# A mixture-of-experts kernel on one core: experts ranked for each set of tokens, weights reloaded in that order, raw token rows

## The chip, the core and the metric

The kernel runs on one core of a Trainium2 chip. Its engines are TensorE (PE, matrix products and transposes), VectorE (DVE), ScalarE (ACT), GpSimd (POOL, which also issues the indirect transfers) and SyncE (SP, which issues nearly all other transfers); sixteen DMA engines carry out what the queues are given. The metric is the time of one execution on the device in microseconds (us), as the median of several runs.

## The reference, cut to what matters

4096 tokens (16 sequences of 256) of width 128 pass four residual steps:

```
x = x + attention(layernorm(x))      # softmax weights summed over m and multiplied by v of the same token
x = x + ffn(layernorm(x))            # layer 1
x = x + mixer(layernorm(x))          # selective scan with 16 states, and the skip term u * D
x = x + ffn(layernorm(x))            # layer 2

ffn: logits = x @ gate_w             # 8 experts
     top 2 of 8, softmax over the two
     h = relu(x @ w1[e])             # 128 -> 512
     y = h @ w2[e]                   # 512 -> 128
     out = sum over the two of weight * y
mixer: y = scan(u, delta, A, B, C) + u * D;  out = y @ W_out + b_out
```

In the attention the softmax weights of a token sum to one over m, so that it reduces to the projection of v. Both layers use the same gate and expert weights. All values are float32.

## The kernel before

**Tiling.** Tokens are worked on in 8 blocks of TB = 512, four tiles of 128 rows each, which stay in SBUF (`xs_[b]`). A layer goes through its blocks in sets: `FIRST = ([0], [1], [2, 3], [4, 5], [6, 7])` in layer 1 and `SECOND = ([0, 1], [2, 3], [4, 5], [6], [7])` in layer 2. For each set, `route` picks two experts per token, works out with a running count (a matmul with a triangle) which slot of which expert each token gets, and scatters the token rows by indirect DMA into a DRAM buffer `slots`. `experts` then goes through the eight experts: it fetches the expert's slots (tile `xs`), transposes them (`xsT`), multiplies with w1 (`up`, PSUM `ps_b` or `ps_B`, then relu into `h`) and w2 (`ps_y`, `yT`), transposes back (`yr`) and stores them in a DRAM buffer `ys`. `collect` gathers for each token its two result rows (`yy`) and adds them to x. The first set of layer 1 has no slots in DRAM: `dealt` builds one-hot matrices and gathers by a matmul. Between the layers stands the mixer; at the end `finish` transposes and writes the output.

**Rooms.** Each expert position r of a set has a fixed room of K x C rows, given in `SLOTS` as (K, C): K is the number of partitions of the tiles `xs` and `yr`, and C the number of rows on each. The PE computes on all K x C columns, used or not. Rooms have to be as large as the number of tokens that any expert in this position gets. `beyond` collects by how much a set overflows, and if any does, a general path computes everything anew after the end. Where K is over 116 or C is 1 (`byrow`), the second product gives rows and needs no second transpose.

**Ranking.** `RANKED = (2,)`: at the first set of layer 2 the experts are ranked by the number of tokens in that set. From then on position r means the expert of rank r; `load_experts` reads its number into a register of SP and loads its weights once for all sets of the layer. In layer 1 the experts have their natural order and equal rooms. `w1_s` and `w2_s` have one buffer for each of the eight positions, 256 KB each.

**Slots in DRAM.** A row's address interleaves the experts: row i of expert e is at i * 8 + e, so a partition's C rows lie apart and each row moves as 512 B.

```
            return t[0 : NE * n * c].rearrange("(p c e) w -> e p c w", e=NE, c=c)[r]
```

**Scaling.** The token rows are normalized and multiplied with their routing weight before they are scattered (tile `row`: one ACT or DVE operation of 128 x 128 for each tile and choice), which relu lets pass. The results are added as they are.

**The order.** The functions do not issue instructions. They record jobs in a `Plan`, each with the tiles it reads and writes, the engines that may do it (`either`), and for transfers an assumed duration (`took`). The string `ORDER` holds a rank for each job and, where there is a choice, the engine; the plan then emits every job in order, with the semaphore waits that follow from it. So all instructions of the profile stand on the one line L772, except the indirect transfers (scatter L880, gather L892), the loads of ranked weights (L934, L940), and filler matmuls (L1705) which are put where the plan expects the PE to be idle. SP is one in-order queue: the loads of weights, the fetches of `xs`, the stores of `ys` and the output stand in it one behind the other, and one that waits holds up the others. POOL is likewise one queue for scatters, gathers and its own arithmetic. `xs` and `yr` have four buffers each (`XS`).

Of the kernel before, what the change touches and what calls it, by code (L numbers as in the profile page):

```python
# [11 lines left out]
BF16 = mybir.dt.bfloat16  # L12
# [7 lines left out]
P = 128  # L20
# [15 lines left out]
        2: ((108, 3),) * 8,  # L36
    },
    {
        "first": ((126, 3), (112, 3), (108, 3), (98, 3), (96, 3), (88, 3), (126, 2), (117, 2)),
        1: ((98, 2), (91, 2), (88, 2), (80, 2), (84, 2), (75, 2), (70, 2), (128, 1)),  # L40
        2: ((126, 3), (117, 3), (110, 3), (104, 3), (108, 3), (96, 3), (90, 3), (126, 2)),
    },
)
RANKED = (2,)
UNIT = 2
JOIN = 2

COLD = 5.0
# [14 lines left out]
    "c-qZZ2V4_p|G(!F2uWCBZ^GVNMD}nMWhmmpRjsY4t)oufI_lQiswi$nt>RvFf>K)%!~%*UB1=HoJFEa1cmE`Jxw{}(`+wi}^LZ0U"  # L63
    "a?kVJZ+?H@-|v>G_^I*=>c6NNCEAl^pxer^W>rkfI9&R;>iv%8rd7`B9lu02joA1NUDGqgsne+5m*>sC|3s_)i)v%K>WE364%f`z"
    "G%9VWd>|BeK0IC08FfuyS$#TV!ssUsJvZ9pw@tBaV2TlOKM(^Ype&9CWvPXsXYyKG+Pu%zXlZI1Sm&A}IY4CALbDer*&iR4gwV&l"
    "%_}jzc_s5zX!X3PvIWf#4x)X!&c}M*s#~aW*_FM4<>R>>-Ss7LRsE&oXUE3!i@n2)%YK;$2Ux%Q=KJd&AzO97EXmqll<=(G$|n86"
    "dYcDRExkEyN=&Uj^@^>Aca=O|2u`0WZ*KkZPp*nx>bjin<VsZC<o=9uRhFUFl+z=MPhNm~zw4pXzFM^_s$-IHUykn8ElEaxc^26-"
    "@4I$-U9_@v4^`W~w0Z1KeP?YmwJLUVr{|Jk*2t*vvi=>escnr%S2%5T@YvyUd1cK_&1T~j6D^|8^}R6ZVc4@5r`2UVu#9lkK^d>j"
    "<5raWMYj1fEzYZOy26KDMUnzv7Ki#3$Js3MGeWdkH_RQX!$+g^SGwX*L0g)m*&ht^hr`B{m+-Z+MtiQ=%kQlyO?ID9`_|x>g>x4a"
    "7{0aWT9KvwE7Mny<Gx<_BC^rwXq|G-%~+*L?XOC-N_X*TlWs>d*t>6dr4MgmZ>V5Cdl#UwvuaJIa7A;6SkO9NyAy2)R#I*_c4irG"  # L70
    "f$}i1aA)c7s#VilXwygk=1!Yh4K5@zA4WBp!hdS2*QXZDe|&PBD<YV-*P?Y!iDl#0qE3S>ix*QK?M<<E=x(XAp(VMh1?XG@R;LUe"
    "^+r5mvX*|O{~BSeh+)#r_1}t5_Zhr&a6Vyi`WybF4oh}yO!N4+5htCOsU-6w+usb|b1Ki@BBPCK;{T?1ty+gYBRIVexWd-=;yaSJ"
    "&s)c$pQk1Mu(kK>{gXydj2^f9i*!A>vkJ$Aory7?vCXs9d*QbqY<=vPD_5viZHRw+xyi_Maei$clW%G}<<Bhkhz`r&MH-;Cg^e&a"
    "U3gYoEtvixd0S^(bWqX_ezZ?DQW4gCxKZW)U-sXiwFV<^9XWugj&I$OH!^<jINSI_Rp(0X8CAy1J2}<+XY8MsQOzx+FI`ck!)UF1"
    "r{3=xWR>+`>d7lshLx35&odZn7Zx}mrDnxJanplDErz>)?7F~R3+C+aA5-pJSJA{omZhmanOZhgkCAfdi0_(u)pB)q^G@34(G14f"
    "eS4#Xe51_BB9U#NK~YP9t>|iZM^tyo*>WS%F&D1MxJN(sPW#RtZCBBJZJ^)!epUT0n_AeiD}P#^{fyO-2NJ+a(?751T|Dt?cbC&s"
    "Vc(n$QTC>HM#at;b;t51I;SD3MmT%!f%h}4>PBvxuFe>3;@b3@A8^VmYfe%~m6J|SeG|jhc2S6Tkp)nnb$DNx$-9k@&62&})9eDh"
    "ScjD#Mm+6S`}*KmrOj)ty&MV-D)rOH_rKCv)^PRbMmOGYj!yTV8??Q`+N`UlY#O%f5B};74O>|C*7x@ozso+too$4EyDPAtJ-2Le"
    "uTEEI%<mI*o7jdlVWH_fj=;E{yK8^RlKf4p9e+HX@qI@>qK&dre+c0=@TMCTa6xyst-wJ;H>2N&$y}<c%!q`U@CUzomIp^G>DPJt"
    "S!x=E$jI-zmAMAtYp?dBF3J<a_^i}!9^FgHm{tEc#Gh9&w{A|0ef5VbPi>8y1=e34J|A%@QR|nJJQv~V+30jzx^DxA@33*RbCs>%"  # L80
    "ef3A`HOopwyjkjeHH}(F$Ieng4b!X;HExa5f1%a}jGt%hF>5F+ZFknJV%x@_61{ioY8P?EddV{*+HUb(fS#Qbt)^2r^(WJ`)UPYu"
    ")JFWl;98WeIb=8Tk2<=R1-&Pa79=`8w;g#um40nvvTte-sCm{D_|vkM$>|}6bRG!cYgMZ0^S*OreBm=TH+%Z~Jcp5~?Y_@P(9st@"
    "2CsX<E{?mh@~%t6aDJ(4L*w;>xy$qNjg9mfd=Ae^*L+-(bAJ8d=)3ycVdKZQ%egm9ODFqhX5N_LFyCI_K3f0nvJ^FDW!RAzPKVo+"
    "&IIVELnF5YsV!Rmvh`YcsoiL^-lwHm!S_vG?p9glT3%@%v(D~K^6D*%ik-FG(>9-*)PGiwXO`l5rF63Hy$X+bo)u_IOW1QRTiI}<"
    "<_VqfqH_^joC>Np-yO~piB@y!^DI<vt(p<a79|+4%EN6Q+BDz2GK+27_hV+{U*BnPFSKTUHNV=Vhjk($xUov;CwT7HHq%es;o@7v"
    "s~x8lM&||AjNuQ<wZ6Bmwd>bY8~1<UXj(W%Ur`$cXWJOv-;lnhYT8?FUx$uYp|x^`un9G&o1Iu;t!dRW&g^Bb=_0hyX(rG0_x5<J"
    "W}lxb*X~)HAE-1pB;BQ^LG!O|{!7wateXuPjy1g47G;AAOE#v|-`IO4l;JX=Le)SmG4aUQQQ6kXA%1z9t<NK0dmq^jAGBJpuKxgd"
    "eXkawFZ5$JMr2mlKB{8c=h)_Zy$KD=PPGs%xvk#g-~MD_9aH;}d%czM@ozmdc5X7%n7k(1V&fu#xkh5jB_tPq;C45@tIXzkaGgr;"
    "`U-V}elJ1K5|2t9!%F4Ie79N)zMgFdqAF5lr;az799pBdl=r?p=s{9t<;`CXoASO{t7VrlBRG@0J_1I0K8Wt`_lI$swmu6BI^+PG"
    "R<t`R#ilQeDPFoWaTfD_W-45&V`fle={DiT+;e$tuyA_JGv2os@98-1FqqaFKEJbL>3+MFs}kA@zjoxM2@bBZ-Zv|~*-qnO412%B"  # L90
    "Hrl?39I;U2Nl)*kc{(>WG8$)ax|gm~8_)17zHBvazRBVuOO~Pjb<fxgT5}Y$rBU13yY<|T>gT@6y{t2fvzNc1KieD~H?c3yIG5%1"
    "EZC;L<sGZu9pMPV16%ccCfxd9<XECrYvkB!<h1ocr=`%<`N@intL=VX)*h7_ooi=p!&4c>U}btmTfv<omWIQ-a$8N>Cfiq*;mz*K"
    "X~Rn9R^2?n+niWz_x`eL{ozpO&1-+YWLh^$VDQqHpSVriI0n@^F|pk#E1}=9&or)NWV*op*e;vXrU5-JJxh-3Fk{-vL_ZWd-(`H2"
    "k@>2&TjXi*rq>P$e>>}7fV!t%UxR&U@8s&d;UV$g>F5|2Zpc2S=4zO^Jm5y+3zK*Htk~qyL5(?+wC+!_Zq6Cy`MkJ=^V`TyeWuXt"
    "&YapiOGBTs*#<0g<ztSzO#Mb4*Oi?TS!SZ4o^E#ZOhD4zQ=R+|Ixbw%HSS}*_Wf~Z>nrHuK4p{B+fH~UE>nKqtaR_P_PR4V=)GIP"
    "!Ikr-C#gjoJ>T&4m`N)*+szxBUi?zstQE)^-*auA<Lrx}7Gn-|ZG9f9D$<H~iw)(J4uc)c&AfL9uaDPpx~_b%G&X4U1Ad5jy|0kt"
# [1679 lines left out]
```

## Time and profile before

| | |
|---|---|
| median of 3 runs | 469.81 us (469.47 to 470.01) |
| the profiled execution | 467.84 us, span 466.1 us, granted clock 0.994 |
| busy, share of span | PE 96%, DVE 74%, ACT 58%, POOL 67% |
| DMA | 55.37 MB, mean 119 GB/s |
| fetches of `xs`, stores of `ys` | 72 and 80 |
| loads of weights | 32 of 256 KB |
| indirect transfers | 120 scatters, 128 gathers |

The profile is one execution, seen by the hardware's profiler. The span runs from the first to the last instruction; the time of the execution has 1.7 us around it. An engine's busy time is the sum of its instructions. Matmuls are pipelined and the ends of their records are modelled, so the mean duration of a matmul is larger than the distance from one start to the next. A float32 matmul leaves two records (two passes over the columns).

### The profile page before, as it was taken

How to read it: one execution, taken by the hardware profiler on the slowest of the kernel's cores; microseconds unless marked ns; L12 is line 12 of the kernel's file. 1: busy time of each engine (PE TensorE's matmuls, PEld its weight loads, DVE VectorE, ACT ScalarE, POOL GpSimd, SP SyncE). 2: the span in 40 equal slices, each digit the busy share in tenths (PEclk: the TensorE clock that was granted, in tenths of full speed). 3: DMA queues.
4: the chain of work that ended last, by engine and by line, in shares of the span. 5: the costliest groups of instructions: out<-in, count | busy, mean ns of one | idle time of the engine just before them, and what ended most of it. 6: DMA issues, size and time to landing. Idle time of an engine off the chain costs nothing.

```text
span 466.1 us, 8797 instructions
## 1 busy us (share of the span) xinstructions
PE 447.0 (96%) x2670; PEld 355.8 (76%) x2670; DVE 345.6 (74%) x1229; ACT 268.3 (58%) x621; POOL 311.8 (67%) x482
## 2 busy tenths in 40 slices
PE   8999999999999999989997999989999999999994
PEld 6889998866766667665665777677678877999993
DVE  4799999778697878999999998996786931223420
ACT  2124443577576854995889496797735534343310
POOL 8188787777673761276866776836785477778662
PEclk9999999999999999999999899999999999999999
DMA  5974234632352423236644322144225333543251
GB/s 155 340 244 135 71 122 134 166 107 66 108 155 67 114 78 96 65 106 195 188 121 142 93 73 76 53 120 132 69 58 146 114 113 90 135 125 91 78 164 45
DMA packets 74917, 55.37 MB, mean 119 GB/s; under 512 B 8184, under 2 KB 66800, under 8 KB 74864
## 3 DMA queue, kind: packets, MB, share of 16 engines
q1 hardware_dynamic: 66640, 38.35, 28.5%
q0 software_dynamic: 7936, 16.27, 12.1%
q8 instruction: 23, 0.38, 0.4%
q14 instruction: 30, 0.25, 0.2%
q10 hardware_dynamic: 288, 0.13, 0.1%
HBM read 28.95 MB, written 25.77 MB: 117 GB/s over the span
## 4 chain that ended last, share of the span: by engine, by line
PE 72%; DVE 16%; ACT 4%; issue 3%; POOL 2%; DMA 1%; POOLq 0%; DVEq 0%; ACTq 0%
PE ps_b L772 25%; PE ps_y L772 24%; PE ps_B L772 21%; DVE x L772 3%; DVE ps_B L772 2%; DVE stats L772 2%; PE ps_y L1705 2%; POOL yy L892 2%; DVE w L772 1%; DMA yy<-ys,of 1%; DVE th L772 1%; ACT th L772 1%; DVE rt L772 1%; ACT decay L772 1%; DVE u L772 1%
## 5 line engine op out<-in xcount | busy, mean ns | idle before, releaser
L892 POOL DMA_INDIRECT yy<-ys,of x128 | 125.5, 980 | 64.4 <-issue 37.2
L880 POOL DMA_INDIRECT slots<-row,to x120 | 120.6, 1005 | 49.5 <-issue 19.4
L772 PE MATMUL ps_y<-h,w_s 128*128 128x324 f32 (+13 forms) x552 | 145.2, 382 | 0.0
L772 PE MATMUL ps_B<-xsT,w_s 128*128 128x324 f32 (+9 forms) x352 | 112.8, 442 | 0.8 <-DVE w L772 0.4
L772 PEld LDWEIGHTS ps_y<-h,w_s 128*128 128x128 f32 x552 | 90.4, 190 | 20.3 <-issue 1.3
L772 PEld LDWEIGHTS ps_B<-xsT,w_s 128*128 128x128 f32 x352 | 61.7, 191 | 23.8 <-issue 3.2
L772 ACT ACTIVATE h<-ps_B 128x648 f32<-128x648 f32 (+9 forms) x62 | 43.8, 707 | 33.5 <-PE ps_B L772 33.1
L772 PE MATMUL ps_b<-xsT,w_s 128*128 128x176 f32 (+9 forms) x288 | 54.8, 316 | 1.2 <-ACT yr L772 1.2
L772 PEld LDWEIGHTS ps_b<-xsT,w_s 128*128 128x128 f32 x288 | 44.1, 190 | 2.7 <-ACT yr L772 1.5
L772 ACT COPY yT<-ps_y 128x324 f32<-128x324 f32 (+14 forms) x52 | 18.8, 362 | 36.0 <-PE ps_y L772 35.2
L772 ACT ACTIVATE th<-later,lneps,ha_s 128x112 f32<-128x112 f32 (+13 forms) x85 | 39.1, 507 | 0.2 <-DVE th L772 0.2
L772 ACT ACTIVATE h<-ps_b 128x352 f32<-128x352 f32 (+9 forms) x47 | 22.3, 474 | 26.0 <-PE ps_b L772 24.1
L772 PE MATMUL ps_b<-ident,yT 128*108 128x128 f32 (+11 forms) x177 | 34.4, 274 | 0.7 <-ACT yr L772 0.7
L772 ACT COPY xsT<-ps_b 128x324 f32<-128x324 f32 (+15 forms) x52 | 19.1, 372 | 26.6 <-PE ps_b L772 25.3
L772 ACT ACTIVATE decay<-delta,nea 128x108 f32<-128x108 f32 (+13 forms) x85 | 31.7, 412 | 2.7 <-DVE delta L772 2.6
L1705 PE MATMUL ps_y<-blank,ones_d 128*128 128x128 f32 x232 | 31.2, 293 | 1.3 <-DVE blank L772 1.3
L772 DVE TENSOR_TENSOR_SCAN w<-decay,ps_B 128x360 f32<-128x360 f32 (+7 forms) x40 | 31.0, 802 | 1.3 <-ACT decay L772 0.5
L1705 PEld LDWEIGHTS ps_y<-blank,ones_d 128*128 128x128 f32 x232 | 30.0, 208 | 1.6 <-DVE blank L772 1.3
L772 ACT COPY yr<-ps_b 108x384 f32<-108x384 f32 (+13 forms) x50 | 21.3, 425 | 16.8 <-PE ps_b L772 16.8
L772 ACT ACTIVATE row<-x,mp,rp 128x128 f32<-128x128 f32 x63 | 28.1, 488 | 3.6 <-DVE rp L772 2.0
L772 PE MATMUL ps_b<-ident,xs 108*128 108x108 f32 (+13 forms) x186 | 29.7, 256 | 0.1
L772 DVE TENSOR_SCALAR h<-ps_B 128x648 f32<-128x648 f32 (+6 forms) x26 | 21.3, 819 | 11.1 <-PE ps_B L772 10.8
(207 smaller groups left out, 792.2 us busy)
## 6 DMA issues: line engine op xcount, KB each, us to landing
w_s<-in_w SPq DMA_DIRECT2D x32, 256.0 KB
xs<-slots SPq DMA_DIRECT2D x27, 162.0 KB
ys<-yr SPq DMA_DIRECT2D x27, 162.0 KB
slots<-blank SPq DMA_DIRECT2D x2, 1280.0 KB
xT<-in_xT SPq DMA_DIRECT2D x8, 256.0 KB
yy<-ys,of POOLq DMA_INDIRECT x128
out_T<-xnT SPq DMA_DIRECT2D x8, 256.0 KB
slots<-row,to POOLq DMA_INDIRECT x120
```

Source lines behind the costliest of these rows:

```text
L772: return lambda: f(*[real(x) for x in a], **{n: real(x) for n, x in k.items()})
L880: inst = nc.gpsimd.indirect_dma_start(out=real(out), out_offset=bass.IndirectOffsetOnAxis(ap=real(rows), axis=0), in_=real(in_), in_offset ...
L892: nc.gpsimd.indirect_dma_start(out=real(out), out_offset=None, in_=real(in_), in_offset=bass.IndirectOffsetOnAxis(ap=real(rows), axis=0),)
L1705: nc.tensor.matmul(out=spare, lhsT=ones_d.real(), rhs=blank.real(), start=True, stop=True,)
```

## The change

- `RANKED` lists eight sets: the three pair sets of layer 1 and all five sets of layer 2. Each ranks its own experts and reloads all sixteen pieces of weights in that order, from register values that one job of SP reads at once.
- `SLOTS` has new rooms, now falling with the rank in the pair sets of layer 1 too. Over all sets there are 18749 rows, 20508 before.
- In DRAM the experts lie one behind the other. A partition's C rows are contiguous, and an address is the base of the expert's room plus the token's count. Tokens beyond a room go to spill rows behind the buffer.
- Token rows are scattered as they are. Weights w1 are centred once (a 128 x 128 matmul with `centre` for each expert, in layer 1) and written to a DRAM copy `w1c`, from where the later loads come; the factor (routing weight times reciprocal deviation) is applied in `collect`, one operation for each tile and choice.
- In the mixer, u is scaled by 2 D in place, the states' contribution is added to its tail, and one product with half of W_out replaces two.
- The one-hots of the first set may also be built on ACT (two operations). The first block's reciprocal deviation is a power on POOL. The plan's idle times count fully in the first 5 us. The assumed duration of fetch and store in the plan is .55 for .9. `ORDER` is a new string for the new list of jobs (left out here).

```diff
@@ -33,19 +33,17 @@
     {
         "first": ((88, 2),) * 8,
         1: ((84, 2),) * 8,
-        2: ((108, 3),) * 8,
+        2: ((108, 3), (99, 3), (94, 3), (90, 3), (89, 3), (87, 3), (128, 2), (122, 2)),
     },
     {
-        "first": ((126, 3), (112, 3), (108, 3), (98, 3), (96, 3), (88, 3), (126, 2), (117, 2)),
-        1: ((98, 2), (91, 2), (88, 2), (80, 2), (84, 2), (75, 2), (70, 2), (128, 1)),
-        2: ((126, 3), (117, 3), (110, 3), (104, 3), (108, 3), (96, 3), (90, 3), (126, 2)),
+        "first": ((126, 3), (109, 3), (107, 3), (98, 3), (96, 3), (88, 3), (123, 2), (115, 2)),
+        1: ((96, 2), (84, 2), (80, 2), (72, 2), (70, 2), (128, 1), (126, 1), (117, 1)),
+        2: ((126, 3), (109, 3), (107, 3), (98, 3), (96, 3), (88, 3), (123, 2), (115, 2)),
     },
 )
-RANKED = (2,)
+RANKED = ((1, 2), (1, 3), (1, 4), (2, 0), (2, 1), (2, 2), (2, 3), (2, 4))
...
@@ -831,6 +846,14 @@
             return lambda *a, **k: either((self.engine, name, a, k))
 
     V, A, G = On("DVE"), On("ACT"), On("POOL")
+
+    def Away(engine):
+
+        def peak(out, ramp, minus, one):
+            engine.activation(out, ramp, AF.Abs, bias=minus)
+            engine.activation(out, out, AF.Relu, bias=one, scale=-1.0)
+
+        return peak
...
-
-    def load_experts(k):
+    w1c = dram("w1c", [NE, P, FF])
+
+    def load_experts(q):
         for r in range(NE):
             into = (w1_s[:, r, :], w2_s[:, ts(r, NFC), :])
-            if k not in RANKED:
+            if not q.ranks:
                 move(into[0], w1[r], 4 * P * FF, took=0.7, turn="weights")
                 move(
                     into[1], w2[r].rearrange("(c p) d -> p c d", p=P), 4 * P * FF, took=0.7,
                     turn="weights",
                 )
+                pw = bank("B", P, FF)
+                matmul(pw, centre, into[0])
+                copy(into[0], pw)
+                move(w1c[r], into[0], 4 * P * FF, took=0.5, turn="centred")
                 continue
-            which, said = orders[k], []
-
-            def first(r=r, out=into[0], which=which, said=said):
-                said.append(nc.sync.value_load(which.real()[0:1, r : r + 1], min_val=0, max_val=NE - 1))
-                nc.sync.dma_start(
-                    out=out.real(), in_=w1[bass.ds(said[0], 1)].rearrange("o p f -> (o p) f")
-                )
-
-            def second(out=into[1], said=said):
+            if r == 0:
+                which, said = orders[q.number], []
+
+                def look(which=which, said=said):
+                    said.extend(
+                        nc.values_load_multi_w_load_instructions(
+                            which.real(), engines=[mybir.EngineType.SP], min_val=0,
+                            max_val=NE - 1,
+                            skip_runtime_bounds_check_because="clamped, and a sum of numbers >= 0",
+                        )[1]
+                    )
+
+                seen = plan.job([("SP", 1.0, look)], [], [which], turn="weights")
+
+            def first(r=r, out=into[0], said=said):
                 nc.sync.dma_start(
                     out=out.real(),
-                    in_=w2[bass.ds(said[0], 1)].rearrange("o (c p) d -> p (o c) d", p=P),
+                    in_=w1c.real()[bass.ds(said[r], 1)].rearrange("o p f -> (o p) f"),
                 )
 
-            plan.job(
-                [("SP", 1.5, first)], [into[0]], [which], late=-4.0 * P * FF, turn="weights"
-            )
-            plan.job(
-                [("SP", 0.6, second)], [into[1]], [which], late=-4.0 * P * FF, turn="weights"
-            )
+            def second(r=r, out=into[1], said=said):
+                nc.sync.dma_start(
+                    out=out.real(),
+                    in_=w2[bass.ds(said[r], 1)].rearrange("o (c p) d -> p (o c) d", p=P),
+                )
+
+            for f, t, of in ((first, into[0], [w1c]), (second, into[1], [])):
+                plan.job(
+                    [("SP", 0.55, f)], [t], of, late=-4.0 * P * FF, turn="weights", after=[seen]
+                )
...
-        rp, mp = small("rp", 2, n), small("mp", 2, n)
         p = p.rearrange("p i n o -> p i (n o)")
-        V.tensor_tensor(rp, p, r.unsqueeze(1).to_broadcast([P, 2, n]), ALU.mult)
-        V.tensor_tensor(mp, p, m.unsqueeze(1).to_broadcast([P, 2, n]), ALU.mult)
-        return small, wide, ohs, p, rp, mp
+        share = new(f"share{n}", [P, 2, n], bufs=3)
+        V.tensor_tensor(share, p, r.unsqueeze(1).to_broadcast([P, 2, n]), ALU.mult)
+        return small, wide, ohs, share
 
...
+            here = k, routed[k - 1].index(blocks)
+            self.ranks = here in RANKED
...
+            ends = [0]
+            for n, c in self.room:
+                ends.append(ends[-1] + n * c)
+            self.starts, self.ends, self.rows = ends[:-1], ends[1:], ends[-1]
             shape = [P, 2, NTT * len(blocks)]
             self.to = new(f"to{len(blocks)}", shape, U32, bufs=3)
             self.of = new(f"of{len(blocks)}", shape, U32, bufs=3)
             if not self.dense:
-                self.slots = self.buffer("slots", TB * NE * len(max(FIRST + SECOND, key=len)), 0)
-            self.ys = self.buffer("ys", NE * MOST, NE * least)[0 : self.rows]
+                self.slots = self.buffer("slots", MROWS + 2 * TB * UNIT, 0)
+            self.ys = self.buffer("ys", MROWS, self.rows)[0 : self.rows]
...
         def part(self, t, r):
 
-            n, c = self.room[r]
-            return t[0 : NE * n * c].rearrange("(p c e) w -> e p c w", e=NE, c=c)[r]
...
+    def bases(kinds):
+
+        if kinds not in tables:
+            t = tables[kinds] = new(f"table{len(tables)}", [P, 2 * len(kinds), NE])
+            for i, room in enumerate(kinds):
+                at = 0
+                for r, (n, c) in enumerate(room):
+                    G.memset(t[:, 2 * i, r : r + 1], float(at))
+                    at += n * c
+                    G.memset(t[:, 2 * i + 1, r : r + 1], float(at))
+        return tables[kinds]
...
     def dealt(q, e, N):
 
-        at, m, xn = hots[q]
+        at, less, xb = hots[q]
         hot = new("u", [P, JOIN, TB], bufs=2).rearrange("p b l -> p (b l)")[:, 0 : NTT * N]
         hot = hot.rearrange("p (t n) -> p t n", n=N)
         pt = bank("b", P, N)
         for t in range(NTT):
-            k = (hot[:, t], ramp.rearrange("p c k -> p (c k)"), at[:, t, e : e + 1], m[:, 0, t, e : e + 1],
-                 ALU.is_equal, ALU.mult)
-            either(("DVE", "tensor_scalar", k, {}), ("POOL", "tensor_scalar", k, {}))
+            count = ramp.rearrange("p c k -> p (c k)")
+            k = (hot[:, t], count, at[:, t, e : e + 1], None, ALU.is_equal)
+            either(
+                ("DVE", "tensor_scalar", k, {}), ("POOL", "tensor_scalar", k, {}),
+                ("ACT", Away, (hot[:, t], count, less[:, t, e : e + 1], one_c), {}),
+            )
         for t in range(NTT):
-            matmul(pt, xn[:, t], hot[:, t], t == 0, t == NTT - 1, turn="enter")
+            matmul(pt, xb[:, t], hot[:, t], t == 0, t == NTT - 1, turn="enter")
         return pt
 
...
-        if q.k in RANKED and q.blocks == routed[q.k - 1][0]:
+        if q.ranks:
             ranking(q, pc[:, n])
-        own = places.get(q.k, number)
+        home = q if q.ranks else q.base
+        lies = places[home.number][q.room] if home else bases((q.room,))
         at = small("rank", n + 1, NE)
-        V.tensor_tensor(at, pc, spread(own if first else q.had, n + 1), ALU.add)
+        V.tensor_tensor(at, pc, spread(lies[:, 0], n + 1), ALU.add)
+        if not q.dense:
+            past = small("past", n, NE)
+            V.tensor_tensor(past, at[:, 0:n], spread(lies[:, 1], n), ALU.is_ge)
+            V.scalar_tensor_tensor(at[:, 0:n], past, BIG, at[:, 0:n], ALU.mult, ALU.add)
         m, f = small("m", 2, n, NE), small("sf", 2, n)
         V.tensor_tensor(
             m, ohs, at[:, 0:n].unsqueeze(1).to_broadcast([P, 2, n, NE]), ALU.mult
@@ -1357,32 +1424,19 @@
         lo = (blocks[0] - q.blocks[0]) * NTT
         idx = q.to[:, :, lo : lo + n]
         if not q.dense:
-            V.tensor_copy(idx, f)
+            V.tensor_tensor(idx, f, spill[:, :, 0:n], ALU.min)
 
         V.tensor_scalar(q.of[:, :, lo : lo + n], f, float(q.rows - 1), None, ALU.min)
-        if last:
-            V.tensor_tensor(beyond[:, q.number], at[0:1, n], limits(q), ALU.subtract)
-        else:
-            V.tensor_copy(q.had, at[:, n])
+        V.tensor_tensor(beyond[:, q.number], at[0:1, n], lies[0:1, 1], ALU.subtract)
         if q.dense:
-            spot(q, blocks[0], pc, ohs, p)
+            spot(q, blocks[0], pc, both)
             return
         for b in blocks:
             lo = (b - blocks[0]) * NTT
             for i in range(2):
-                r = new("row", [P, NTT, P], bufs=ROW)
-                for t in range(NTT):
-                    w, m = (v[:, i, lo + t : lo + t + 1] for v in (rp, mp))
-                    either(
-                        ("ACT", "activation", (r[:, t, :], xs_[b][:, t, :], AF.Identity),
-                         dict(bias=m, scale=w)),
-                        ("DVE", "tensor_scalar", (r[:, t, :], xs_[b][:, t, :], w, m, ALU.mult,
-                                                  ALU.add), {}),
-                        turn="row" if t == 0 else None,
-                    )
                 for t in range(NTT):
                     scatter(
-                        q.slots, idx[:, i, lo + t : lo + t + 1], r[:, t, :], f"in{q.name}",
+                        q.slots, idx[:, i, lo + t : lo + t + 1], xs_[b][:, t, :], f"in{q.name}",
                         "a slot has one token",
                     )
 
@@ -1396,7 +1450,7 @@
                 pt = dealt(q, r, N)
             else:
                 x = new("xs", [P, CMAX, P], bufs=XS)[0:K, 0:C]
-                move(x, q.part(q.slots, r), 4 * N * P, took=0.9, turn="fetch")
+                move(x, q.part(q.slots, r), 4 * N * P, took=0.55, turn="fetch")
                 pt = bank("b", P, N)
                 for c in range(C):
                     transpose(
...
-            move(q.part(q.ys, r), yr, 4 * N * P, took=0.9, key=f"out{q.name}")
+            move(q.part(q.ys, r), yr, 4 * N * P, took=0.55, key=f"out{q.name}")
 
     def collect(q, b):
 
@@ -1450,7 +1504,11 @@
             y = new("yy", [P, NTT, P], bufs=ROW)
             for t in range(NTT):
                 gather(y[:, t, :], q.ys, q.of[:, i, lo + t : lo + t + 1])
-            product(xs_[b], xs_[b], y, ALU.add)
+            for t in range(NTT):
+                V.scalar_tensor_tensor(
+                    xs_[b][:, t, :], y[:, t, :], q.share[:, i, lo + t : lo + t + 1],
+                    xs_[b][:, t, :], ALU.mult, ALU.add,
+                )
 
-    wsd_s = new("wsd_s", [P, P])
-    V.tensor_scalar(wsd_s, wso_s, dsk_s, None, ALU.mult)
+    skip2 = new("skip2", [P, 1])
+    V.tensor_scalar(skip2, dsk_s, 2.0, None, ALU.mult)
     wsh_s = new("wsh_s", [P, P])
     V.tensor_scalar(wsh_s, wso_s, 0.5, None, ALU.mult)
 
@@ -1647,11 +1705,13 @@
         for i, b in enumerate(blocks):
             so = bank("b", P, TB)
             sos = new("sos", [P, NTT, P])
-            matmul(so, wsd_s, u[:, i], True, False, hold=[sos])
-            matmul(
-                so.rearrange("p (s l) -> p s l", l=L)[:, :, L - KM : L], wsh_s,
-                whole[:, NSEQ * i : NSEQ * i + NSEQ], False, True,
+            either(
+                ("ACT", "activation", (u[:, i], u[:, i], AF.Identity), dict(scale=skip2)),
+                ("DVE", "tensor_scalar", (u[:, i], u[:, i], skip2, None, ALU.mult), {}),
             )
+            own = slice(NSEQ * i, NSEQ * i + NSEQ)
+            product(ends[:, own], ends[:, own], whole[:, own], ALU.add)
+            matmul(so, wsh_s, u[:, i], hold=[sos])
             A.activation(sos.rearrange("p t d -> p (t d)"), so, AF.Identity, bias=bso_s)
             pt = transposed(sos, xs_[b])
             V.tensor_tensor(xs_[b], xs_[b], pt.rearrange("p (t d) -> p t d", d=P), ALU.add)
@@ -1682,8 +1742,8 @@
             for bs in units(blocks):
                 before(bs)
                 route(q, bs)
-            if blocks == sets[0] and (k == 1 or k in RANKED):
-                load_experts(k)
+            if q.ranks or q.number == 0:
+                load_experts(q)
             experts(q)
             behind(blocks, q)
 
```

## Prediction

> **What bounds the kernel now.** I read the totals first, then the DMA part, then the costliest groups, then the waits, then busy time by stretch.
>
> ```profile
> PE 447.0 (96%) x2670; PEld 355.8 (76%) x2670; DVE 345.6 (74%) x1229; ACT 268.3 (58%) x621; POOL 311.8 (67%) x482
> ...
> DMA packets 74917, 55.37 MB, mean 119 GB/s; under 512 B 8184, under 2 KB 66800, under 8 KB 74864
> ...
> q1 hardware_dynamic: 66640, 38.35, 28.5%
> q0 software_dynamic: 7936, 16.27, 12.1%
> ...
> PE 72%; DVE 16%; ACT 4%; issue 3%; POOL 2%; DMA 1%; POOLq 0%; DVEq 0%; ACTq 0%
> ```
>
> TensorE (PE) is busy 96% of the span and 72% of the chain of waits; the 16 DMA engines are busy 41% on average. The groups with shapes kept apart say what the PE does:
>
> ```profile
> L772 PE MATMUL ps_y<-h,w_s 128*128 128x324 f32 x216 | 71.0, 443 | 0.0
> L772 PE MATMUL ps_B<-xsT,w_s 128*128 128x324 f32 x216 | 69.3, 442 | 0.6 <-DVE w L772 0.4 <-DVE var L772 0.3
> L1705 PE MATMUL ps_y<-blank,ones_d 128*128 128x128 f32 x232 | 31.2, 293 | 1.3 <-DVE blank L772 1.3
> ```
>
> Each f32 matmul has two records (two passes). The means overlap; from start to start a pass takes 273 ns for 324 columns, 429 for 512, so 0.842 ns a column. Hence a slot row costs the PE 16 passes, 16 x 0.842 = 13.5 ns, and about 1.7 ns of transposes (16.2 + 19.1 us over 20508 rows). L1705 is filler, 25.7 us by its steps.
>
> Busy time by stretch (columns: length; PE, weight loads, DVE, ACT, POOL; clock, DMA share, GB/s), cut at the pair sets of layer 1 and of layer 2:
>
> ```profile
> 82.00:252.00 170.00, 165.77 (x849) 114.76 (x848) 146.57 (x418) 126.02 (x282) 109.77 (x141) 1.00 0.41 117
> 252.00:396.00 144.00, 141.02 (x816) 108.19 (x817) 109.69 (x355) 92.73 (x201) 97.60 (x132) 0.99 0.33 97
> ```
>
> The PE is full in both, and its longest waits on another engine, two on a copy, are this short (total, times, longest):
>
> ```profile
> PE ps_b L772 <- ACT yr L772: 1.9, 2, 1.2
> ```
>
> So columns taken away there shorten the span, until something else is full.
>
> **PE terms.** Rows of slots summed over the sets fall from 20508 to 18749: 3 x 391 in the layer-1 pairs, 336 in the layer-2 pairs, 250 in the singles. 1759 x 15.2 ns = 26.7 us less. The skip term drops 360 columns in 8 blocks, 8 x 360 x 2 x 0.842 = 4.8 less. Centring w1 adds 8 matmuls of 512 columns, 6.9 more, at worst all on the path of the first 82 us (the PE had 4 us free before 40). Fillers go from 116 to 127, put where there is nothing else: 0. Sum -24.7: the span 466.1 becomes 441.4. The layer-1 pair stretch becomes 170 - 18 - 2 = 150 us and the layer-2 one 144 - 5 - 2 = 137, if nothing else stops them. The 8 serial gathers and the output at the end (447 to 466) stay.
>
> **DVE, ACT, POOL.** DVE loses 57 row scalings at 0.353 (20.1) and 20 block additions at 0.705 (14.1), and gains 128 scaled additions, nearest row `x<-ps_B,rstd,x` at 344 ns (44.0, or 36 at the 281 of a 128-wide read) and seven more rankings of some nine operations at about 0.2 (13). Net 10 to 20 more in 345.6, most of it in the two stretches, where DVE was busy 146.57 of 170 and 109.69 of 144. That gives about 98% of a 150 us stretch in the worst case: I take 2 us, bounds -1 and +6. ACT sheds some 28 us of row scalings and takes back 11 (skip scaling, one-hots): no cost, at 58%. POOL loses 12 products and gains 80 one-element memsets in the beginning; its scatters no longer wait for rows. Zero, bounds -3 and +2.
>
> **Weights and SP.** Eight sets reload 16 x 256 KB, one did before: 112 transfers and 29 MB more, plus eight 256 KB stores. Each issue took SP 0.35 to 0.4 us, and SP mostly waited for others, so 16 issues are 6 us beside a set of 50. A load waits for the last expert that used the same weights, and behind it on SP stand the next fetches of token rows and stores of results. The cover is the order, seven expert positions ahead; I take 0, bounds 0 and 3 us a set (256 KB landed in 2.7 to 3.1 us unhurried).
>
> **The transfers of the slots: the term that decides.** The change also changes the row counts K that are the partition count of every fetch of xs and store of ys. The trace holds a record for each 4-byte signal by which an engine reports its share. Per transfer they are 14 for K=84, 11 for 88, 12 for 108, 16 for 112, 13 for 117 (or one more, which comes early), in each case the largest divisor of K up to 16. Over all transfers: the 152 fetches and stores make 1992 by this pattern, 68 others 16 each, 10 small ones 8 each; 1992 + 1088 + 80 = 3160. With 32 from another queue, 640 small data packets, 384 loads of 384 B and 3968 signals of the software queue this is 8184, exactly the row "under 512 B". Sixteen engines each would have made 520 more. So all K of the kernel before have a divisor of 11 to 16 and run wide. The new K do not:
>
> - layer-1 pairs: 108, 99, **94, 90, 89, 87**, 128, **122** give 12, 11, 2, 15, 1, 3, 16, 2 engines (90 is wide);
> - layer-2 pairs: 126, **109, 107**, 98, 96, 88, **123, 115** give 14, 1, 1, 14, 16, 11, 3, 5.
>
> That is the pattern carried to K which the trace does not show; the far bound is that they run on 11 to 16 like the others. With four fetches of 12 engines in flight (84.4 us) the hardware queue never had more than about 13 packets open, and 17 to 18 in the weight loads: the transfers share the same twelve engines, not different ones. So one engine serves a part of every transfer, and its bytes for one set can be summed, each transfer being K x C x 512 B over its engines.
>
> Layer-1 pair set: 13.8 + 13.8 + 72.2 + 9.2 + 136.7 + 44.5 + 8.2 + 62.5 = 361 KB, twice for fetch and store, 722; layer-2: 13.8 + 167.4 + 164.4 + 10.8 + 9.2 + 12.3 + 42.0 + 23.6 = 443.5, twice is 887. Evenly spread over 16 it would be 141 and 150. A 2048 B packet took 84 ns in the median (24.4 KB/us) and 100 in the mean (20.5); 512 B packets in the mean 17.8. I take 22, as the single engine has little company. Then layer 1: 32.8, weights 262 KB 11.9, 32 scatters and gathers 6.4, together 51.1 a set, 153 for three, against 150 of PE: +3. Layer 2: 40.3 + 11.9 + 6.4 + output 1.5 = 60.1, 180 for three, against 137: +43. With both nearly in series at set ends (a 109-row fetch alone is 167/22 = 7.6 us, against 2.7 to 3.1 for 108 rows before, and its store is what the gathers wait for) I add 8. At 24.4 it is 0 + 26; at 20.5 15 + 57; 17.8 would be 37 + 83, which I take as too slow.
>
> Span: 441.4 + 2 + 46 + 8 = 497; the profiled execution lay 1.7 over its span (467.84 against 466.1) and the median 2.0 over that (469.81): 501. Own range of this case 470 (at 24.4) to 540.
>
> The Trainium skill, "DMA: Bandwidth & Descriptors", section "Why a DMA increments its semaphore by 16 and not by 1", states the same divisor rule for hardware-queue transfers, with 127 partitions on one engine, and that the lowest-numbered engines are taken. It speaks against this change: by it the sum is the 501 above, while by row counts alone ("nearly equal rows, nearly equal time") it would be 447. The trace agrees on the divisors (3160 signals); that engine numbers are the lowest no view here shows.
>
> **The rivals.**
> 1. *Transfers stay hidden.* The narrow ones use different engines, or four buffers of xs hide 8 us beside five-us experts. For it: no wait of the PE for a fetch in before, and descriptors of 1 to 1.5 KB for 512 B. Against: the thirteen open packets. Then 466.1 - 24.7 + 3.7 = 445, with the DVE's 2 us 447; faster. Chance 0.13.
> 2. *DVE becomes the bound* on top of rival 1: +6, 453, still faster. Chance 0.04.
> 3. *Reloads come late.* In eight sets the weights arrive after the PE wants them; from 24.7 / 8 = 3.1 us each it cancels the gain. At 3.1, 470 (same); at 4, 477. The 16 loads of a set stand in SP's order between fetches and stores. Chance 0.03.
> 4. *Overflow.* If a set's tokens exceed their rows, the general path computes everything a second time. The rooms fit the routing with 3 rows to spare: 0.01.
>
> **How the numbers follow.** The narrow-transfer case has 0.79, all of it slower. Faster (by over 0.2%, which is about what a measurement of this kernel can tell from no change): 0.17; same 0.02; slower 0.81. Range: 470 to 540 holds the first case but for a few hundredths and leaves 0.21 out; I reach down to 450, which takes in rival 2 and the partly hidden cases.
>
> **What would show it.** In the profile of after: PE busy below 85% (the work of 441 less the gaps, over 497); PE waits ending on xsT or on fetches in the layer-2 pair sets; signals of a 109-row transfer one, its landing 7 to 9 us after issue; DMA share not much higher than before. If the landing stays near 3 us, or PE remains at 95%, the forecast is wrong. If landings are long and the PE is nonetheless full, the buffers hide them (rival 1).

## Result and the profile after

The changed kernel takes 541.67 us in the median (539.9 to 543.5, 4 runs), the kernel before 469.91 in runs beside it: ratio 1.1526, 95% interval 1.1479 to 1.1572. The forecast was 501 us with a range of 450 to 540: the side was right, the size too small, the time lies 1.7 us above the range. The profiled execution took 539.9 us with a span of 538.2, at a mean granted clock of 0.912 (0.994 before).

Of the page: the totals, PE and its granted clock in 40 slices (tenths), and the DMA queue of the fetches and stores:

```profile
PE 450.8 (84%) x2668; PEld 366.5 (68%) x2668; DVE 358.2 (67%) x1331; ACT 248.7 (46%) x576; POOL 289.4 (54%) x503
...
PE   8899998988981999378986999478995599498994
...
PEclk9999999998996799769997899769998599879998
...
q1 hardware_dynamic: 77372, 66.43, 40.7%
```

PE fell from 96% to 84% of a longer span, as the forecast said (below 85%). Its gaps lie in about the places where the clock row shows 5, 6 or 7: that the clock goes down with the gaps is something the forecast did not have. The DMA queue moved 28 MB more (the reloads) and is still far from full. The chain of waits of this profile breaks off close to its end and is not used.

Who waited for whom (total, times, longest), in after:

```profile
PE ps_b L784 <- DMA xs<-slots: 34.6, 8, 8.0
DVE x L784 <- DMA yy<-ys,of: 48.0, 25, 12.2
PE ps_B L784 <- DVE w L784: 11.2, 2, 10.9
PE ps_B L784 <- DVE pieces L784: 8.9, 1, 8.9
```

Before, no wait of PE on a transfer stood among its waits, and the second kind of wait was 17.4 us. One fetch, first from SP's side and then from PE's (start, duration, idle before):

```profile
340.58 4.17 SPq L784 DMA_DIRECT2D xs<-slots  x3
```

```profile
340.97 1.02 PE L784 MATMUL ps_b<-u,wsh_s 128*128 128x512 f32 x2
345.70 0.86 PE L784 MATMUL ps_b<-ident,xs 126*128 126x126 f32 x3 [3.71 <-DMA xs<-slots]
352.62 0.60 PE L784 MATMUL ps_b<-ident,xs 109*128 109x109 f32 x2 [6.05 <-DMA xs<-slots]
```

SP began the fetches of 126, 109 and 107 rows at 340.6, 341.0 and 341.3 us. The first landed after 5.0 us, the 109 rows after 11.5, the 107 rows after 18.2. From 344 to 352 the packet records hold 1.1 packets of the hardware queue open in the mean, where the split version below has 9.4 in the same stretch (with other jobs under way): as far as the packets tell, one engine works, and everything else on that queue stands behind it. The landing records show one late signal for 109, 107 and 89 rows, two for 94 and 122, three for 87 and 123, five for 115, just as the divisors said.

To see where 72 us went I cut both executions into the same four parts and divided PE's time three ways: work (each matmul at the step that it has at full clock, filler included), loss to half clock (the clock records give its stretches) and gaps (the rest).

| part | before: us | work / clock / gaps | after: us | work / clock / gaps |
|---|---|---|---|---|
| start (0 to 82, both) | 81 | 64.7 / 0 / 16.1 | 81 | 67.2 / 0 / 13.7 |
| layer 1 pair sets (82 to 252; 277) | 170 | 156.9 / 0 / 13.2 | 195 | 139.3 / 13.3 / 42.4 |
| layer 2 pair sets (to 396; 464) | 144 | 133.3 / 1.7 / 8.8 | 195 | 135.0 / 10.6 / 49.2 |
| the rest | 70 | 61.1 / 0.1 / 8.9 | 66 | 51.9 / 2.8 / 11.7 |

(A part ends with the first matmul that starts after its border, so that the long wait at 463 counts to layer 2.) Summed: work 416.0 to 393.4, clock 1.8 to 26.7, gaps 47.0 to 116.9. The saving of PE work is there to the microsecond, 22.6 with 2.5 more of filler, so 25.1 against the forecast 24.7. Gaps took 70 back and the clock 25.

### The profile page after: what moved, and what is told of

It is laid out like the page before. It is cut to its first block, busy times and chain, and to the rows that moved or that the text cites. A ratio compares the mean times of both kernels' runs of the same rounds, so it can differ in the third digit from the quotient of the medians.

```text
span 538.2 us, 9251 instructions
## 1 busy us (share of the span) xinstructions
PE 450.8 (84%) x2668; PEld 366.5 (68%) x2668; DVE 358.2 (67%) x1331; ACT 248.7 (46%) x576; POOL 289.4 (54%) x503
## 3 DMA queue, kind: packets, MB, share of 16 engines
q0 software_dynamic: 7936, 16.27, 10.2%
## 5 line engine op out<-in xcount | busy, mean ns | idle before, releaser
L903 POOL DMA_INDIRECT slots<-x,to x120 | 116.9, 974 | 59.4 <-issue 25.2
L784 PE MATMUL ps_y<-h,w_s 128*128 128x168 f32 (+17 forms) x496 | 129.6, 382 | 0.9 <-ACT yT L784 0.6
L784 PE MATMUL ps_B<-xsT,w_s 128*128 128x324 f32 (+11 forms) x288 | 95.8, 456 | 11.2 <-DVE w L784 11.2
L784 DVE SCALAR_TENSOR_TENSOR x<-yy,share,x 128x128 f32<-128x128 f32 x128 | 43.3, 344 | 48.1 <-DMA yy<-ys,of 48.0
L784 PE MATMUL ps_b<-xsT,w_s 128*128 128x168 f32 (+12 forms) x352 | 71.2, 329 | 1.9 <-DVE h L784 1.8
L784 PE MATMUL ps_b<-ident,xs 84*128 84x84 f32 (+19 forms) x174 | 33.1, 271 | 34.6 <-DMA xs<-slots 34.6
L784 ACT ACTIVATE h<-ps_B 128x756 f32<-128x756 f32 (+11 forms) x50 | 33.7, 673 | 59.6 <-PE ps_B L784 55.0
L784 ACT ACTIVATE th<-later,lneps,ha_s 128x112 f32<-128x112 f32 (+14 forms) x85 | 39.7, 506 | 0.4 <-DVE th L784 0.4
L784 PE MATMUL ps_y<-w_s,h 128*126 128x128 f32 (+4 forms) x264 | 39.1, 284 | 0.1
L784 PEld LDWEIGHTS ps_y<-w_s,h 128*126 128x126 f32 (+4 forms) x264 | 35.0, 194 | 2.0 <-ACT h L784 0.6
```

Source lines behind the costliest of these rows:

```text
L784: return lambda: f(*[real(x) for x in a], **{n: real(x) for n, x in k.items()})
L903: inst = nc.gpsimd.indirect_dma_start(out=real(out), out_offset=bass.IndirectOffsetOnAxis(ap=real(rows), axis=0), in_=real(in_), in_offset ...
```

## Experiments

Theory: the time goes to transfers whose row count has no large divisor, carried by one to five engines that all transfers share. Rivals: the eight rankings and reloads, or the tighter order that goes with them, cost it; or narrow transfers hurt only beside reloads.

**Splitting the narrow transfers.** Nothing else is changed: the same rooms, jobs, order, rankings, reloads. The transfers of eight row counts are issued in two parts.

```diff
+    PARTS = {94: 90, 89: 88, 87: 84, 122: 120, 109: 108, 107: 105, 123: 120, 115: 112}
+            nc.sync.dma_start(out=o[0:n], in_=i[0:n])
+            nc.sync.dma_start(out=o[n:K], in_=i[n:K])
```

> The kernel after with each fetch and store of 94, 89, 87, 122, 109, 107, 123 or 115 rows issued as a wide transfer and a small rest. Asked again since on two chips the kernel before itself took over 630 us, with long waits for nothing that the profile shows. Theory (few DMA engines carry the narrow transfers and hold up all others): about 447 us (443 to 456), granted clock over 0.98, no PE wait on a fetch over 2 us. Rival (rankings, eight reloads or the tighter order): over 520. Both: 480 to 500.

Measured: 461.48 us (457.23 to 464.62), ratio to before 0.9764 (0.9696 to 0.9832). 80 of the 541.67 us are gone, and the kernel is faster than before, by 1.7 to 3.0%. Its totals, and busy time in the two pair parts (length; PE, weight loads, DVE, ACT, POOL; clock, DMA share, GB/s):

```profile
PE 427.3 (93%) x2668; PEld 350.2 (76%) x2668; DVE 357.4 (78%) x1331; ACT 248.1 (54%) x576; POOL 290.9 (63%) x503
```

```profile
82.00:243.70 161.70, 151.56 (x888) 119.77 (x886) 136.60 (x405) 106.47 (x247) 100.51 (x129) 0.98 0.63 190
243.70:394.90 151.20, 143.54 (x838) 110.03 (x838) 127.06 (x428) 92.70 (x197) 102.11 (x141) 1.00 0.56 173
```

```profile
82.00:277.00 195.00, 161.92 (x886) 126.87 (x885) 136.50 (x405) 106.60 (x247) 99.31 (x128) 0.89 0.53 157
277.00:471.80 194.80, 154.07 (x838) 117.11 (x838) 127.63 (x428) 93.60 (x198) 104.74 (x146) 0.88 0.45 136
```

The second pair of lines is after, for comparison. Both have the same 2668 matmul records in the same order, so the borders are the same two matmuls: the one that starts at 277.0 us in after starts at 243.7 here, the one at 471.8 at 394.9. The two parts take 33 and 44 us less, and the clock is back at 0.98 and 1.00. In my division: work 393.4 (the same), clock 2.8 instead of 26.7, gaps 61.9 instead of 116.9. So the rankings, the reloads and the order are not what costs the 80 us: with all of them in place the kernel is faster than before. The loss of 25 us of clock is a consequence of the waits, since no edit touched the clock. The time is 5 us over the theory's range: of the saving of 24.7 only 8.5 arrives. Gaps are 61.9 where before had 47.0, many short ones of PE for DVE and ACT (the longest 3.3 in total), DVE being busy 137 of 162 and 127 of 151 us. Whether DVE causes them was not tried.

**One layer at a time**, in one job with after itself (the lines against the split kernel):

```diff
-                if K in PARTS and True:
+                if K in PARTS and q.k == 1:   # or q.k == 2, for fetch and store
```

> The kernel after, unchanged, as the base for the three that follow on the same chip. 541.7 us where the kernel before takes 470; where that takes 635 to 645, waits of other kinds cover a part of the loss, and I expect 660 to 710.

> The kernel after with split transfers in layer 2 alone; layer 1's pair sets stay narrow. By 19.5 KB a us on one engine, layer 1 loses 21 us (722 / 19.5 = 37, with weights 13 and indirect transfers 7 a set, 57 against 50, three sets) and layer 2 66 (45.5 + 13.4 + 8.7 = 67.6 against 45.7). So layer 2 has the larger share: 45 to 65 us less than after_same. Rival (both layers alike, as each has one to two transfers on one engine): 30 to 45 less.

> The kernel after with split transfers in layer 1 alone: by the same sum 15 to 30 us less than after_same; the two halves should add up to 79 where the kernel before takes 470.

After: 540.59 us. Split in layer 2 alone: 500.28 (40.3 less). Split in layer 1 alone: 504.53 (36.1 less). Together 76.4, about the 79 of both: the two parts add up. But they are alike, which was the rival; my sums of 66 and 21 were both wrong. Between the same matmuls as above, layer 1 took 162 us where it was split and 195 where it was not, layer 2 158 and 191. The waits tell why. First layer 1 split, layer 2 narrow:

```profile
PE ps_b L784 <- DMA xs<-slots: 30.1, 6, 7.9
DVE x L784 <- DMA yy<-ys,of: 33.4, 24, 3.9
```

Then layer 2 split, layer 1 narrow:

```profile
PE ps_B L784 <- DVE w L784: 11.8, 3, 11.3
PE ps_b L784 <- DMA xs<-slots: 4.1, 4, 2.1
DVE x L784 <- DMA yy<-ys,of: 47.3, 27, 12.9
```

And with both split (the waits of PE for fetches are below the listed ones):

```profile
DVE x L784 <- DMA yy<-ys,of: 25.7, 22, 3.9
```

In layer 2 the narrowest row counts, 109 and 107, are at positions 2 and 3 (123 and 115 stand at 7 and 8): PE waits for the fetch at the beginning of a set. In layer 1 the narrow ones are 3, 5, 6 and 8. The four buffers hide the fetches there (4.1 us of waits), but the last stores of a set are narrow: in after, 122 rows landed after 10.6 and 10.4 us, and the wide store of 128 rows after 8.2 and 8.4, as it stands behind narrow ones. The gathers wait for these stores. After the first set this goes as follows:

```profile
155.19 1.79 SPq L784 DMA_DIRECT2D ys<-yr  x1
166.53 0.97 POOL L915 DMA_INDIRECT yy<-ys,of  x1 [17.78 <-DMA w_s<-w1c]
171.29 0.95 POOL L784 TENSOR_TENSOR du<-delta,u 128x360 f32<-128x360 f32 x1
172.27 0.49 DVE L784 TENSOR_SCALAR u<-u,skip 128x512 f32<-128x512 f32 x1 [16.28 <-POOL du L784]
174.51 1.78 PE L784 MATMUL ps_B<-xsT,w_s 128*128 128x282 f32 x3 [10.86 <-DVE w L784]
```

The store of 122 rows, issued at 155.19, landed at 165.74. The first gather started 0.8 us later (the name in its bracket is of a load that landed after that store). `du`, a product of the mixer, stood behind four gathers in POOL's queue, DVE waited for `du`, and PE for DVE's scan. After the second set the 122 rows landed at 219.75 and the first gather started at 220.60; DVE's addition waited 12.2 us for it, `pieces` stood behind the addition in DVE's queue, and PE waited 8.9 us for `pieces`. What decides in layer 1 is not how much the engine has to carry in a set, but who is last.

**Is the half clock a loss of its own?** Fillers keep PE busy where it waited for six fetches of layer 2:

```diff
+    HOLD = {(2, 0, 2): 8, (2, 2, 0): 16, (2, 2, 1): 26, (2, 4, 0): 24, (2, 4, 1): 26, (2, 6, 0): 34}
+            extra = 0 if summing or way[0] != "PE" else held.get(job.n, 0)
+            for _ in range(extra + (0 if summing or idle < 0.5 else int(idle / 0.26))):
```

> The kernel after with 134 filler matmuls before six fetched experts of layer 2, where the PE waited 2.5 to 8.4 us and then ran at half clock. If the half clock is part of the loss by itself: 8 to 15 us less than after_same. If the shared engine sets the pace: within 3 us of it, at a higher clock. On a chip where the fetches are not what the PE waits for there, the fillers cost up to their 30 us.

544.06 us, 3.5 more than after_same. Over the same 187 us of layer 2:

```profile
277.00:464.00 187.00, 172.71 (x1042) 137.70 (x1041) 129.49 (x428) 92.81 (x196) 100.66 (x141) 0.95 0.44 134
```

The clock there is 0.95 instead of 0.89, half-clock time over the whole run 67 us instead of 92. Yet from the same first matmul of layer 2 (277.6 us here, 275.7 in after_same) to the transposes of 123 rows in the last pair set it took 179.9 us in both. The first single set then began 5 us later than in after_same (199.7 against 194.5 us): its rows had landed at 471.7, but the 34 fillers before them ran until 477.2. So a faster PE gains nothing in these sets: the transfers set the pace, and the half-clock loss there is hidden beneath them. The 25 us of clock must not be added to the waits as a second cause. For the 13.3 us of it in layer 1 this was not tried.

**Width alone, in the kernel before**, which has one reload and scaled rows, in layer 2 only:

```diff
-        "first": ((126, 3), (112, 3), (108, 3), (98, 3), (96, 3), (88, 3), (126, 2), (117, 2)),
+        "first": ((126, 3), (109, 3), (107, 3), (98, 3), (96, 3), (88, 3), (123, 2), (117, 2)),
-        2: ((126, 3), (117, 3), (110, 3), (104, 3), (108, 3), (96, 3), (90, 3), (126, 2)),
+        2: ((126, 3), (117, 3), (109, 3), (103, 3), (108, 3), (96, 3), (90, 3), (126, 2)),
```

> The kernel before with only layer 2's pair rooms made narrow (first set 109, 107 and 123 for 112, 108 and 126; the other two 109 and 103 for 110 and 104). Layer 2's narrow transfers cost the kernel after 40 us. If eight reloads are no condition for it, 490 to 515; less than 40 more, since a set here has 13 us of weights fewer on the shared engine: 20 to 40 over the kernel before. If the reloads are a condition: within 6 us of the kernel before.

531.62 us (531.29 to 531.96), ratio 1.1320 (1.1299 to 1.1341): 62 us slower for 30 rows fewer (18 in the first set, 6 in each of the others; the 34 of an expectation below is a slip). Its longest waits of PE:

```profile
PE ps_b L772 <- DMA xs<-slots: 33.5, 8, 7.3
```

Reloads are no condition. That it is more than expected has two parts. From the first fetch of layer 2 to the first fetch of a single set it took 46 us longer (a 109-row fetch of 512 B pieces lands after 10.9 to 12.1 us). And what follows took some 17 us longer: the plan, which works its order out of the ranks and of the assumed durations at build time, came to another sequence with other rooms, and put in 94 more filler records, 10 us of them in these last sets. So the size is not clean; the sign and the waits are.

**Rounding the rooms up**, the natural repair:

```diff
-        2: ((108, 3), (99, 3), (94, 3), (90, 3), (89, 3), (87, 3), (128, 2), (122, 2)),
+        2: ((108, 3), (99, 3), (96, 3), (90, 3), (90, 3), (88, 3), (128, 2), (126, 2)),
-        2: ((126, 3), (109, 3), (107, 3), (98, 3), (96, 3), (88, 3), (123, 2), (115, 2)),
+        2: ((126, 3), (110, 3), (108, 3), (98, 3), (96, 3), (88, 3), (126, 2), (117, 2)),
```

(also for `first`; and `byrow` from 118 on, so that the jobs stay the same ones).

> The kernel after with rooms rounded up to row counts with a divisor of 11 to 16; 108 more slot rows, 1.6 us of PE work, and 48 fewer issues than the split transfers (461.5 where before took 470.0). 458 to 465 if only the width counts; below 459 if the second issues cost something.

511.6 us (510.68 to 513.91), a miss by 47. Its waits of PE and its filler:

```profile
PE ps_B L784 <- ACT h L784: 2.9, 3, 1.3
```

```profile
L1765 PE MATMUL ps_y<-blank,ones_d 128*128 128x128 f32 x598 | 77.0, 285 | 3.4 <-DVE ones_d L784 1.3
```

The wait of PE for fetches is gone here too, and the loss to half clock is 7.7 us; DVE still waits 53.3 us for gathers. But there are 598 filler records, 254 in after: 38.5 of the 39.2 us by which its work exceeds after's. The string `ORDER` belongs to the old rooms; with new ones the same ranks gave another sequence, in which the plan sees long idle times and fills them. The run says that wide rooms take the waits away; it says nothing on their price, since the order changed with them. A size in this kernel can't be tried alone.

**Four other jobs.** In these the kernel before took 630 to 646 us, with long waits for nothing that the profile shows, so that their times stand only against before in the same job; the kernel after itself was not run there. The same kernels there: split 630.0 against 633.7 and 643.8 against 646.0; narrow 671.1, 680.8, 680.9 and 670.4 against 633.7, 646.0, 644.7 and 629.7, so 35 to 41 us slower each time; rounded rooms 636.8 against 633.7 and 653.7 against 644.7; fillers 679.6 and 693.2 against 633.7 and 644.7; split in layer 2 alone 663.9 against 644.7. What was expected of the first four, before that was known:

> The kernel after with nothing changed but this: each fetch and store of 94, 89, 87, 122, 109, 107, 123 or 115 rows is issued as two transfers, a wide one (90, 88, 84, 120, 108, 105, 120, 112 rows) and the few rows left. Theory (few DMA engines carry the narrow transfers and hold up all others): the loss goes and the saving of PE columns appears, about 447 us (443 to 456), granted clock over 0.98, no PE wait on a fetch over 2 us. Rival (the rankings, the eight reloads or the tighter order cost the time, and transfers are long only because these queue): stays over 520. If both share: between, say 480 to 500.

> The kernel after with its rooms rounded up to row counts with a divisor of 11 to 16 (94 to 96, 89 to 90, 87 to 88, 122 to 126, 109 to 110, 107 to 108, 123 to 126, 115 to 117): 108 more slot rows in all, so 1.6 us more PE work than after, still one transfer each. Theory: about 448 us (443 to 457), like the split transfers. Rival (the second issue of the split, not the width, would be what changes things; or the reloads are the cause): over 520.

> The kernel before, with only the rooms of layer 2's pair sets made narrow: first set 112 to 109, 108 to 107, 126 to 123 (C 2); the other two 110 to 109 and 104 to 103. 34 fewer slot rows, 0.5 us less PE work; one ranking, one reload, scaled rows as before. Theory: the engine that all transfers share then has 429 and twice 394 KB in each direction a set, 2 x 405 / 19 = 43 us and 9 of others against 48 of PE, with a reload of 13 us once and waits at the beginning of each set: slower, 490 to 520 us. Rival (narrow transfers alone are hidden by the four buffers, and it takes eight reloads beside them): 468 to 475.

> The kernel after with filler matmuls (8, 16, 26, 24, 26 and 34 of 0.22 us) put before six fetched experts of layer 2 where the PE waited 2.5 to 8.4 us for the fetch and then ran at half clock. No transfer changes. If the half clock after each wait is part of the loss: half-clock time falls from 97 us to about 55 and the time by some 12 us, to 525 to 535. If the transfers alone set the pace there, the PE is faster and only waits longer for the next one: 539 to 544, at a higher clock.

Of the same split kernel (643.8 us against 646.0) and of the same narrow one (680.8 against 646.0, then 680.9 against 644.7, then 670.4 against 629.7):

> The kernel of split_all once more, on another chip: there the kernel before itself took 633.7 us, with long waits for nothing that the profile shows, so that nothing on the widths follows from it. Theory (few DMA engines carry the narrow transfers and hold up all others): about 447 us (443 to 456), granted clock over 0.98, no PE wait on a fetch over 2 us. Rival (rankings, eight reloads or the tighter order): over 520. Both: 480 to 500.

> The kernel of narrow_before once more, on another chip. The kernel before with only layer 2's pair rooms made narrow (first set 109, 107 and 123 for 112, 108 and 126; the other two 109 and 103 for 110 and 104). Theory: 490 to 520 us. Rival (the four buffers hide narrow transfers as long as there are no eight reloads): 468 to 475.

> The kernel before with only layer 2's pair rooms made narrow (first set 109, 107 and 123 for 112, 108 and 126; the other two 109 and 103 for 110 and 104); one ranking, one reload, scaled rows as before. Theory: 490 to 520 us, with a granted clock of 0.94 to 0.97. Rival (the four buffers hide narrow transfers as long as there are no eight reloads): 468 to 475.

> The kernel before with only layer 2's pair rooms made narrow (first set 109, 107 and 123 for 112, 108 and 126; the other two 109 and 103 for 110 and 104); one ranking, one reload, scaled rows as before. Run as the only kernel of its job. Theory: 490 to 520 us, with a granted clock of 0.94 to 0.97. Rival (the four buffers hide narrow transfers as long as there are no eight reloads): 468 to 475.

Of the rounded rooms (653.7), the fillers (693.2) and the split in layer 2 alone (663.9), all against 644.7:

> The kernel after with rooms rounded up to row counts with a divisor of 11 to 16 (94 to 96, 89 to 90, 87 to 88, 122 to 126, 109 to 110, 107 to 108, 123 to 126, 115 to 117), each fetch and store one transfer. 108 more slot rows, 1.6 us of PE work. If width is the cause, as with the split transfers (461.5 us): 455 to 465, below these where the second issue of the split costs something. If the split itself did it: over 520.

> The kernel after (541.7 us) with filler matmuls (8, 16, 26, 24, 26 and 34 of 0.22 us) before six fetched experts of layer 2, where the PE waited 2.5 to 8.4 us and then ran at half clock. No transfer changes. If the half clock after each wait is part of the loss: half-clock time falls from 97 us to about 55, and the time by some 12 us, to 525 to 535. If the transfers alone set the pace: 539 to 544 at a higher clock.

> The kernel after with the split transfers in layer 2 alone; layer 1's pair sets keep 94, 89, 87 and 122 rows on 2, 1, 3 and 2 engines. By the measured 19.5 KB a us on one engine, layer 1 has 722 / 19.5 = 37 us of slots, 13 of weights and 7 of scatters and gathers a set, 57 against 50 of PE, so some 21 us for three sets, and the clock's share on top: 461.5 + 25 to 35 = 485 to 500. If layer 1 stays hidden (my forecast had +3): 462 to 468. If it is layer 1 that mattered most: over 510.

No absolute figure was met. The signs agree with the runs above: narrow rows make before slower, and with split transfers after is as fast as before (the same within 2% in both).

## Why the forecast was right on the side and wrong on the size

- **PE terms: right.** 25.1 us less work, forecast 24.7. Centring w1 cost nothing visible: the first 82 us took 81 in both.
- **Which transfers are narrow, and that one engine serves them in turn: right**, shown by the signals, by the 1.1 open packets and by the split. The Trainium skill's page "DMA: Bandwidth & Descriptors" has the divisor rule in "Why a DMA increments its semaphore by 16 and not by 1", and every landing of a narrow row count here agrees with it. That it is always the lowest-numbered engines no record here names.
- **The engine's rate: about right.** In layer 2 the 107-row fetch (164 KB) landed 7.0 to 8.8 us after the 109-row one ahead of it, 18.7 to 23.5 KB a us, against the 22 that I took; a store of 109 rows with nothing ahead of it took 9.3 us, against 7.6 without start and end. Over all engines 1536 B packets took 75.0 ns in the mean, 20.5 KB a us (2048 B ones 19.8; two expectations took 19.5). With 20.5 the forecast's sum is 15 + 57 and about 527 us, nearer, but by shares that are wrong the other way. (Its case at 17.8 should read 40 + 86 for 37 + 83; nothing rests on it.)
- **Layer 2: the addition right, its base too low.** Forecast 43 over 137 and a share of the 8; measured 195 us, 44 over the 151 of the split. That the 43 is met so closely is in part luck: it supposed an engine that is never idle, but by the packet records nothing of the hardware queue was under way in 35 of the 195 us.
- **Layer 1: the step that failed.** "51.1 a set, 153 for three, against 150 of PE: +3" compares two totals, as if the engine could work ahead at all times. Measured: 195 us, 33 more than with split transfers, and nothing of the hardware queue was under way in 33 of the 195. The narrow stores come last in these sets and stand in series with the gathers and the mixer. The "8" for such series, for both layers, was an estimate without a row beneath it, and it was the term that mattered.
- **The base: too low by 14 us.** 150 and 137 supposed that each us of PE work saved comes off the span. With split transfers the parts take 162 and 151, and the kernel 461.5 where the forecast's rival of hidden transfers had 447. The 2 us for DVE and the like were too little; what fills the rest stays open.
- **The clock: not in the forecast.** 26.7 us of PE work were lost at half clock, but by the fillers nothing would have come off the time of layer 2's pair sets without it. "TensorE: Matmul & The Clock Gate" in the Trainium skill (Part 1, "What's actually happening") says that the clock halves after an idle window of some 3.4 us. The half-clock stretches of after last 3.4, 6.8, 10.2, 13.7 or 17.1 us (the one at its end apart), multiples of such a window. But the window before need not be idle throughout: before 8 of its 12 stretches, PE had no matmul in only 1.0 to 2.5 of the last 3.4 us.
- Of the rivals, late reloads are refuted by the split: all 112 of the added loads are in it, and it is faster than before.

## What to carry to other kernels

Look at the divisors of a transfer's row count (its partitions) before its bytes: three rows fewer on 112 turned a fetch of 3 us into one of 11 to 12, and what stood behind it on the queue waited along. If a row count must stay as it is, issue the bulk and the few odd rows as two transfers; here that was worth 80 of 541.7 us and gave the fastest kernel of all, 461.5. And when a shared resource is nearly full, don't compare totals: ask which of its transfers comes last before a dependent step, and add that in series.

## What the runs showed of the hardware that was not expected

- After waits of 2.1 to 10.9 us, mostly for fetches and for the mixer, PE ran at half clock for 3.4 to 17.1 us: 97 us of such time in after, 7.5 in before, 14.0 in the split version, whose PE instructions are those of after.
- Where transfers set the pace the cost of that was hidden: in the filler run 25 us less of it left layer 2's pair sets at 179.9 us.
- In the jobs with before at 630 to 646 us, engines stood still for 5 to 25 us and more at a time. Late loading of instructions would be one guess, but the trace of split_again does not bear it out: of 57 such standstills 6 ended within 1.5 us after a packet of the instruction queues, where chance alone would give 8. What is behind them stays open.
